# Layer 2 of a four-layer graph stack: the logit row and the transposed attention matrix go through DRAM and VectorE instead of TensorE

## The chip, the core and the metric

The kernel runs on one core of a Trainium2 chip, in float32. A core has five engines with a queue each, worked through strictly in order: TensorE (PE, matrix products; PEld is its weight load), VectorE (DVE), ScalarE (ACT), GpSimd (POOL) and SyncE (SP), which here does nothing but issue DMAs. The metric is the device time of one execution in microseconds (us); less is better.

## The reference, cut to what matters

`x` is 128 graphs ("batches") of 128 nodes by 512 features; `adj` is one 128 by 128 matrix for all. Each layer is `x = layernorm(x + layer(x))`:

```python
# layer 0: max over nodes of relu(A + C - A')           (adj as both weights)
# layer 1: 8-head attention masked by adj, projections Wq Wk Wv Wo
# layer 2: graph attention
h  = einsum('bnc,cf->bnf', x, W)
s1 = einsum('bnf,f->bn', h, a1);  s2 = einsum('bnf,f->bn', h, a2)
e  = leaky_relu(s1[:, :, None] + s2[:, None, :], 0.2) * mask      # mask is adj
att = softmax(e, axis=2)
out = elu(einsum('bij,bjf->bif', att, h) + beta * h)
# layer 3: norm_adj @ (x @ weight) + bias
```

In layer 2, `s1` is one number per row node and `s2` one number per column node. A column of 128 numbers lies across the 128 partitions of the on-chip memory, so `s2` has to be turned into a row that every partition holds. And the 128 by 128 matrix `att + beta * I` has to be transposed before TensorE can multiply by it. These two turnings are what the change is about.

## The kernel before, in words

The work on each batch is cut into named steps (a table `STEPS`, line 185). Each step has an engine, a cost that the author gave it, the steps that must precede it, and the buffers it takes. A planner in the kernel (`list_order`, line 74) walks through all steps of all 128 batches with these costs and writes down one order of work. On TensorE it takes the step that can start first, and among those the one of lowest `rank` (line 392): the batch number plus a lag given by stage (`LAG`, line 369), with a few exceptions (`LEAD`). The chip then follows this order, engine by engine; steps on different engines are tied by semaphores alone. So the order is fixed when the program is built, and each engine waits where its next instruction is not ready, however much else could be done.

Batches go in pairs (even and odd). The projections Q, K, V (layer 1), Y (layer 1's output), U (layer 2's weight) and Z (layer 3's weight) of a pair are computed with seven products in place of eight, steps `QP1` to `QP7` and so on, each about 0.9 us of TensorE; sums of blocks for them are formed by GpSimd (`US1` to `US4`), and results are evacuated from the accumulators by VectorE and ScalarE (`QU2`, `KU3`, `UC22`). The last six batches use the plain product (`YF0`, `YF1`, ...). `A` is layer 0's product, `SC` the attention scores and `O` the weighted values of layer 1, `GT` layer 2's product with the attention matrix, `NX` layer 3's with `norm_adj`. `MX1`/`MX2` write the normed batch to DRAM and read it back in another order of 32 by 32 blocks, which VectorE then transposes in place (`TX`); `MS1`/`MS2`/`TS` do the same with the attention weights of layer 1.

Layer 2 of a batch `b` runs in this order:

- `Y1`, `Q1`, `P1`, `AP1`: the layer norm behind layer 1 (VectorE, ScalarE, GpSimd, ScalarE).
- `L` (VectorE, line 1062): two dot products per node give the columns `s1` and `s2`.
- `E` (TensorE, line 1076): a transpose against the identity of `s2`, broadcast along the row, leaves the row of `s2` on all partitions, in an accumulator bank.
- `EZ` (ScalarE, line 1082): adds `s1`, twice: once into a buffer `z` in on-chip memory, once in place in the bank.
- `E1` (VectorE), `EE` (ScalarE), `E2` (VectorE): leaky relu, mask, maximum; exponential and its sum; division and `beta * I`.
- `BT` (TensorE, line 1115): transposes the matrix into a bank. `BE` (ScalarE, line 1120) copies it to a buffer `bT`.
- `GT` (TensorE, line 1125): eight matrix instructions; then `GE`, the sums, `UP1` to `UP7`, and the elu.

`E` and `BT` need a bank of the accumulator pool `ps` (five banks). The buffer counts are in `POOLS`: one `z`, two `bT`, two `e`, three pairs of `x2` (layer 1's result).

Of the kernel before, what the change touches and what calls it, by code (L numbers as in the profile page):

```python
# [8 lines left out]
F32 = mybir.dt.float32  # L9
AF = mybir.ActivationFunctionType  # L10
# [3 lines left out]
P = 128  # L14
S = 32
Q = P // S
# [55 lines left out]


def list_order(steps, rank, pools, n):
    todo = {(s, b) for s in steps for b in range(n) if steps[s].batches(b)}
    missing, users, ready = {}, {}, {}
# [12 lines left out]
    while todo:  # L89
        best = None  # L90
        for k in can:
            s = steps[k[0]]
            t = max(ready[k], free.get(s.engine, 0.0), free.get("port", 0.0) if s.port else 0.0)
            for i, (p, _) in enumerate(s.buffers(k[1])):
                n_taken = len(taken[p]) + (i and p == s.buffers(k[1])[i - 1][0])
                if n_taken >= pools[p]:
                    for r in taken[p][n_taken - pools[p]]:
                        t = max(t, ends.get(r, 1e9) + SIGNAL)
            if t >= 1e9:
                continue  # L100
            if s.engine != "PE":
                key = (t, ready[k] - s.soon - (s.rush if k[1] < 4 else 0.0), k, t)
            elif mode and s.mode:
                near = CLOSE + (CLOSE if s.mode == mode else 0.0)
                key = (max(t - AWAIT, free["PE"]), rank(*k) - near, k, t)
            else:
                key = (t, rank(*k), k, t)
            if best is None or key < best:
                best = key
# [63 lines left out]
def normed(b):  # L173
# [3 lines left out]
POOLS = {  # L177
    "ps": 5, "sc": 3, "x": 4, "xB": 2, "xT": 2,
    "qT": 2, "kT": 1, "v": 2, "s": 1,
    "sB": 2, "oT": 1, "x2": 3, "z": 1, "e": 2, "bT": 2, "gT": 1, "m": 1, "x3": 2,  # L180
    "nx": 1, "dx": 8, "dp": 2, "S": 2, "SX": 2, "u": 2, "uL": 1,
    "t0": 3, "t1": 3, "t2": 3, "t3": 3, "r": 3,
}
# [46 lines left out]
    "P1": Step("POOL", 0.58, "Q1", soon=20, batches=normed),  # L230
    "AP1": Step("ACT", 1.03, "P1", "P1*", soon=20),
    "L": Step("DVE", 1.45, "AP1", "LOG2a@", "LOG2b@", soon=20, port=True),
    "E": Step("PE", 0.12, "L", takes={"ps": ("E1",)}),
    "EZ": Step("ACT", 0.42, "E", takes={"z": ("E1",)}, soon=20),
    "E1": Step("DVE", 1.0, "EZ", takes={"e": ("BT",)}, soon=20),
    "EE": Step("ACT", 0.42, "E1", soon=20),
    "E2": Step("DVE", 0.57, "EE", soon=20, port=True),
    "BT": Step("PE", 0.12, "E2", takes={"ps": ("BE",), "bT": ("GT",)}),
    "BE": Step("ACT", 0.2, "BT", soon=20),
    "GT": Step("PE", 0.89, "BE", "GT-1", takes={"ps": ("GE",), "gT": ("U+",)}),  # L240
    "GE": Step("ACT", 0.5, "GT", soon=20),
    "UE": Step("ACT", 0.55, "U1", soon=20),
# [110 lines left out]
for n, need, weights, end, out in (  # L353
# [13 lines left out]


LAG = {
    "A": 0.692, "QP4": 9.305, "QP6": 13.674, "KP4": 14.013, "QP1": 14.257, "VP6": 14.264,  # L370
    "QP7": 14.272, "KP7": 14.275, "QP2": 14.757, "KP6": 14.810, "QP5": 16.139,
    "KP1": 16.167, "SC": 16.245, "QP3": 16.292, "KP5": 16.483, "KP2": 16.726, "KP3": 16.957,
    "VP1": 17.469, "VP7": 17.505, "VP2": 17.717, "VP4": 17.842, "VP3": 17.872,
    "VP5": 17.926, "YP4": 18.786, "YP5": 19.034, "O": 20.374, "YP3": 21.316, "YP1": 21.809,
    "YF1": 21.819, "YP2": 21.908, "YP6": 21.936, "YP7": 22.056, "E": 22.106, "UF1": 22.207,
    "YF0": 22.911, "BT": 23.043, "UP1": 23.223, "GT": 23.299, "UP4": 23.974, "UP5": 24.264,
    "UP3": 24.731, "UP2": 24.753, "UP6": 24.814, "UP7": 24.920, "UF0": 25.326,
    "ZP7": 25.453, "ZF0": 25.880, "NX": 25.925, "ZP4": 26.433, "ZP2": 26.459, "ZP6": 26.533,
    "ZP1": 27.158, "ZP3": 27.371, "ZP5": 27.563, "ZF1": 28.500,
}  # L380

LEAD = {
    "V55": -0.01, "NX59": 0.02, "GT60": -2.5, "V60": 0.06, "BT61": 0.07, "Z61": -1.43,
    "BT62": -0.59, "GT63": 1.52, "NX63": -0.85, "A4": 3.8, "O0": 1.06, "O1": -0.73, "GT2": 0.02,
    "V1": -0.26,
}


BOTH = range(128)


def rank(name, b):
    if name not in LAG:
        return -1.0
    stage = name[0] if name[1:2] in "PF" else name
    if name in ("SC", "O") and b in BOTH:
        b |= 1
    return b + LAG[name] - LEAD.get(f"{stage}{b // 2}", 0.0)


@with_exitstack
def kernel(
# [20 lines left out]
    nc = tc.nc  # L423
# [11 lines left out]
    dram = ctx.enter_context(  # L435
        tc.tile_pool(name="dram", bufs=2, space=bass.MemoryType.DRAM)
    )
# [4 lines left out]
    def mm_tile(name):  # L442
        return psum.tile([P, 512], F32, tag="ps", name=name, bufs=POOLS["ps"])

    def tr_tile(name):
        return mm_tile(name).rearrange("p (c f) -> p c f", c=C)

    def buf(tag, shape, b):
        return work.tile(shape, F32, tag=tag, name=f"{tag}_{b}", bufs=POOLS[tag])
# [73 lines left out]
    ident = const.tile([P, P], F32, tag="ident", name="ident")  # L523
# [103 lines left out]
    scores, probs, sums, dp, sT, v, oT = {}, {}, {}, {}, {}, {}, {}  # L627
    x2, s12, e, bT, gT, m, x3, nx = ({} for _ in range(8))
# [444 lines left out]
                accum_out=s12[b][:, i : i + 1],  # L1073
            )

    def E(b):

        ps = tr_tile(f"ps_e_{b}")
        nc.tensor.transpose(ps[:, 0, :], s12[b][:, 1:2].to_broadcast([P, P]), ident)
        e[b] = ps  # L1080

    def EZ(b):
        z = e[b][:, 0, :]
        s1 = s12.pop(b)[:, 0:1]
        z_sb = buf("z", [P, P], b)
        nc.scalar.activation(z_sb, z, AF.Identity, bias=s1)
        nc.scalar.activation(z, z, AF.Identity, bias=s1)
        e[b] = z, z_sb

    def E1(b):  # L1090
# [21 lines left out]
        )  # L1112
        e[b] = t

    def BT(b):
        ps = tr_tile(f"ps_bT_{b}")
        nc.tensor.transpose(ps[:, 0, :], e.pop(b), ident)
        bT[b] = ps

    def BE(b):  # L1120
        t = buf("bT", [P, P], b)
        nc.scalar.copy(t, bT[b][:, 0, :])
        bT[b] = t

    def GT(b):

# [84 lines left out]
    def OUT(b):  # L1211
# [3 lines left out]
    do |= {f.__name__: f for f in (  # L1215
        Q0, Q1, Q2, Q3,
        LD, ST0, A, R, P0, AP0, MX1, PX, PT, PTE, MX2, RL, C1, TX, SC, M0, M, SM1, EXP, SMR, SMN, MS1, MS2, TS, O, OE,
        Y1, P1, AP1, L, E, EZ, E1, EE, E2, BT, BE, GT, GE, U1, UE, U2, UP, U3, P2, AP2, NX, NE,
        C3, Z1, P3, AP3, OUT,
    )}  # L1220
    for name in FETCH:
# [55 lines left out]
```

## Time and profile before

| | |
|---|---|
| Time, median of 3 runs (lowest, highest) | 3055.86 us (3053.38, 3056.8) |
| Span of the profiled execution, first to last instruction | 3055.6 us |
| PE busy | 3021.9 us, 21062 instructions |
| DVE busy | 2350.8 us, 5379 instructions |
| ACT busy | 2215.0 us, 7240 instructions |
| POOL busy | 1624.7 us, 1907 instructions |
| Bytes moved by DMA, mean rate | 313.19 MB, 102 GB/s |
| Start of the score blocks of two successive pairs, late in the run | 2243.10 and 2289.79 us |

The profiled execution's span is 0.3 us below the median of the runs, so the sums can be made against either. Busy time is the time in which an engine has an instruction under way. Matrix instructions are pipelined: one that is "0.27 us" long from its first to its last moment can be followed by the next after 0.11 us. What a matrix instruction costs TensorE is therefore read from the distance between its start and the start of the next, not from its duration. In a timeline line, consecutive instructions of one kind are drawn together ("x8").

### The profile page before, as it was taken

How to read it: one execution, taken by the hardware profiler on the slowest of the kernel's cores; microseconds unless marked ns; L12 is line 12 of the kernel's file. 1: busy time of each engine (PE TensorE's matmuls, PEld its weight loads, DVE VectorE, ACT ScalarE, POOL GpSimd, SP SyncE). 2: the span in 40 equal slices, each digit the busy share in tenths (PEclk: the TensorE clock that was granted, in tenths of full speed). 3: DMA queues.
4: the chain of work that ended last, by engine and by line, in shares of the span. 5: the costliest groups of instructions: out<-in, count | busy, mean ns of one | idle time of the engine just before them, and what ended most of it. 6: DMA issues, size and time to landing. Idle time of an engine off the chain costs nothing.

```text
span 3055.6 us, 61911 instructions
## 1 busy us (share of the span) xinstructions
PE 3021.9 (99%) x21062; PEld 2706.8 (89%) x21062; DVE 2350.8 (77%) x5379; ACT 2215.0 (72%) x7240; POOL 1624.7 (53%) x1907
## 2 busy tenths in 40 slices
PE   7999999999999999999999999999999999999998
PEld 5888988988989989989889899898898898999987
DVE  6878777787787787877777877878778777777774
ACT  4677777777777776777777777777777777667675
POOL 4336555455455555554554655545545545556544
PEclk8999999999999999999999999999999999999999
DMA  7523333233233332332332323323323333223221
GB/s 198 179 87 124 89 107 111 85 116 104 84 118 98 97 114 88 111 108 83 118 102 91 117 88 107 111 87 115 104 84 118 98 97 109 86 77 97 70 84 38
DMA packets 235276, 313.19 MB, mean 102 GB/s; under 512 B 27729, under 2 KB 157649, under 8 KB 234961
## 3 DMA queue, kind: packets, MB, share of 16 engines
q1 hardware_dynamic: 233184, 308.19, 31.9%
q8 instruction: 167, 2.74, 0.4%
q10 hardware_dynamic: 1776, 1.05, 0.2%
q14 instruction: 149, 1.21, 0.1%
HBM read 174.92 MB, written 134.22 MB: 101 GB/s over the span
## 4 chain that ended last, share of the span: by engine, by line
PE 94%; DVE 3%; DMA 2%; ACT 1%; issue 0%; SPq 0%; POOL 0%; ACTq 0%; POOLq 0%; DVEq 0%
PE py_Q L737 6%; PE py_K L737 5%; PE py_U L737 5%; PE py_Y L737 5%; PE py_V L737 5%; PE py_Z L737 5%; PE ps_s L945 4%; PE pz_Q L737 4%; PE px_K L737 4%; PE pz_K L737 4%; PE ps_o L1024 4%; PE ps_nx L1181 4%; PE px_Q L737 4%; PE ps_gT L1130 4%; PE px_Z L737 4%; PE pz_V L737 4%
## 5 line engine op out<-in xcount | busy, mean ns | idle before, releaser
L1195 POOL TENSOR_TENSOR x<-x,b_bc 128x512 f32<-128x512 f32 x128 | 162.8, 1273 | 601.7 <-PE ps_nx L1181 601.6
L672 ACT ACTIVATE x<-x,off,rstd 128x512 f32<-128x512 f32 x512 | 416.8, 814 | 17.1
L981 ACT ACTIVATE s<-s,mx 128x128 f32<-128x128 f32 x1024 | 396.1, 390 | 36.7 <-DVE mx L975 36.6
L640 DVE BATCH_NORM_STATS2 st<-x 128x6 f32<-128x512 f32 x512 | 346.6, 677 | 13.9 <-POOL x L1162 7.7
L995 ACT ACTIVATE s<-s,sm 128x128 f32<-128x128 f32 x1024 | 313.3, 389 | 18.5 <-DVE sm L990 7.8
L667 POOL TENSOR_TENSOR rstd<-rstd,neg_half 128x2 f32<-128x2 f32 (+1 forms) x265 | 182.3, 688 | 149.9 <-ACT rstd L653 149.7
L1162 POOL TENSOR_TENSOR x<-x,x 128x512 f32<-128x512 f32 x128 | 163.2, 1275 | 142.4 <-DVE rs L1108 75.4
L716 POOL TENSOR_TENSOR SX_V<-xT 128x256 f32<-128x256 f32 x128 | 93.7, 732 | 272.2 <-PE py_Y L737 243.8
L1034 ACT COPY nx<-ps_nx 128x512 f32<-128x512 f32 x128 | 74.9, 585 | 215.9 <-PE ps_nx L1181 215.6
L1066 DVE SCALAR_TENSOR_TENSOR junk<-x,wa_bc 128x512 bf16<-128x512 f32 x256 | 207.1, 809 | 14.8 <-ACT x L672 4.0
L796 DVE TENSOR_TENSOR x<-py_U,u_U 128x256 f32<-128x256 f32 x183 | 77.6, 424 | 151.8 <-PE py_U L737 151.3
L981 ACT ACTIVATION_READ_ACCUMULATOR s<-s,mx 128x1 f32 x1024 | 193.5, 189 | 0.0
L959 DVE TENSOR_TENSOR s<-ps_s,mask 128x512 f32<-128x512 f32 x256 | 169.1, 682 | 9.3 <-DMA dp<-s 5.8
L896 POOL TENSOR_TENSOR x<-x,bo_bc 128x512 f32<-128x512 f32 x128 | 160.3, 1274 | 14.5 <-DVE bo_bc L593 8.1
L716 POOL TENSOR_TENSOR S_U<-gT 128x256 f32<-128x256 f32 x122 | 93.0, 762 | 128.8 <-ACT gT L1034 128.6
L1016 DVE STREAM_TRANSPOSE sB<-sB 128x1024 f32<-128x1024 f32 x128 | 157.9, 1234 | 0.8 <-DMA sB<-dp 0.8
L737 PEld LDWEIGHTS px_K<-xT,wk_sb 128*128 128x128 f32 x1024 | 133.8, 192 | 27.3 <-issue 23.6
L671 ACT ACTIVATE off<-off,rstd 128x1 f32<-128x1 f32 x512 | 145.6, 284 | 15.4 <-POOL rstd L667 15.2
L975 DVE TENSOR_REDUCE mx<-s 128x8 f32<-128x1024 f32 x128 | 153.5, 1199 | 0.3
L945 PE MATMUL ps_s<-kT,qT 64*128 64x128 f32 x2048 | 148.8, 285 | 0.0
L945 PEld LDWEIGHTS ps_s<-kT,qT 64*128 64x128 f32 x2048 | 124.3, 187 | 23.4 <-issue 23.1
L854 PE MATMUL ps_a<-x,adjT 128*128 128x512 f32 x256 | 134.4, 609 | 6.5 <-DMA x<-in_x 6.5
(190 smaller groups left out, 9151.1 us busy)
## 6 DMA issues: line engine op xcount, KB each, us to landing
dp<-s SPq DMA_DIRECT2D x128, 512.0 KB, 2.9
sB<-dp SPq DMA_DIRECT2D x512, 128.0 KB, 3.1
x<-in_x SPq DMA_DIRECT2D x128, 256.0 KB, 3.4
dx<-x SPq DMA_DIRECT2D x128, 256.0 KB, 4.4
x<-dx SPq DMA_DIRECT2D x64, 512.0 KB, 4.0
out_x<-x SPq DMA_DIRECT2D x128, 256.0 KB, 2.0
xB<-dx SPq DMA_DIRECT2D x496, 64.0 KB, 2.0
wo_sb<-in_L_gnn_Wo SPq DMA_DIRECT2D x5, 256.0 KB, 3.7
```

Of the source, the lines that this page charges most:

```text
L640: nc.vector.bn_stats(st, t)
L667: nc.gpsimd.tensor_tensor(r, r, neg_half.to_broadcast([P, r.shape[1]]), ALU.pow)
L672: nc.scalar.activation(dst, src, AF.Identity, bias=shift, scale=scale)
L716: nc.gpsimd.tensor_tensor(s[:, i], x, y, op)
L737: nc.tensor.matmul(to, lhsT=one, rhs=two, start=(new and k == 0), stop=(k == 1), skip_group_check=True,)
L945: nc.tensor.matmul(scores[b][par][:, c, :], lhsT=qT[b][rows, c, cols], rhs=kT[b][rows, c, cols], start=True, stop=True,)
L959: nc.vector.tensor_tensor(by_head(probs[b])[:, par * C : (par + 1) * C], scores[b][par].rearrange("p h (q s) -> p h q s", s=S), mask.rearr ...
L981: nc.scalar.activation(s[:, :, h], s[:, :, h], AF.Exp, bias=mx[:, h : h + 1], accum_out=sums[b][:, h : h + 1],)
L995: nc.scalar.activation(s[:, :, h], s[:, :, h], AF.Identity, scale=sm[:, h : h + 1])
L1066: nc.vector.scalar_tensor_tensor(junk, x2[b][:, b % 2], 1.0, wa_bc[i], op0=ALU.mult, op1=ALU.mult, accum_out=s12[b][:, i : i + 1],)
L1162: nc.gpsimd.tensor_tensor(t, t, x2.pop(b)[:, b % 2], ALU.add)
L1195: nc.gpsimd.tensor_tensor(t, t, b3_bc, ALU.add)
```

## The change

`E` and `BT` are taken out of TensorE.

- The row of `s2` now goes through DRAM: `ER1` writes the column to a DRAM tile of 128 numbers (one 4-byte element per partition), and `ER2` reads it back with every partition reading all 128 numbers, straight into `z`. Both are DMAs issued by SP. `EZ` still makes its two copies with `s1` added; it now reads `z` and takes its accumulator bank itself.
- The attention matrix goes through DRAM too: `BM1` writes it out (64 KB), `BM2` reads it back with four DMAs, each of which fills 32 partitions with 4 by 32 by 32 blocks in an order in which only the blocks themselves remain to be transposed (runs of 32 numbers, 128 bytes). `BE` is now VectorE's 32 by 32 transpose, in place, instead of ScalarE's copy out of a bank.
- The ranks are new: three tables by stage, for the first eight batches (`EARLY`), the last eight (`LATE`) and the rest (`LAG`), and no exceptions by pair. With them the order of nearly all steps changes.

```diff
-    "E": Step("PE", 0.12, "L", takes={"ps": ("E1",)}),
-    "EZ": Step("ACT", 0.42, "E", takes={"z": ("E1",)}, soon=20),
-    "E1": Step("DVE", 1.0, "EZ", takes={"e": ("BT",)}, soon=20),
+    "ER1": Step("SP", 0.4, "L", takes={"de": ("ER2",)}, dma=(1.6, 0.2)),
+    "ER2": Step("SP", 0.4, "ER1", takes={"z": ("E1",)}, dma=(1.6, 0.4)),
+    "EZ": Step("ACT", 0.72, "ER2", takes={"ps": ("E1",)}, soon=20),
+    "E1": Step("DVE", 1.0, "EZ", takes={"e": ("BM1",)}, soon=20),
...
-    "BT": Step("PE", 0.12, "E2", takes={"ps": ("BE",), "bT": ("GT",)}),
-    "BE": Step("ACT", 0.2, "BT", soon=20),
+    "BM1": Step("SP", 0.4, "E2", takes={"db": ("BM2",)}, dma=(1.6, 0.3)),
+    "BM2": Step("SP", 1.9, "BM1", takes={"bT": ("GT",)}, dma=(3.4, 1.0)),
+    "BE": Step("DVE", 0.24, "BM2", soon=20),
...
-    stage = name[0] if name[1:2] in "PF" else name
-    if name in ("SC", "O") and b in BOTH:
-        b |= 1
-    return b + LAG[name] - LEAD.get(f"{stage}{b // 2}", 0.0)
+    lag = (EARLY if b < 8 else LATE if b >= 120 else LAG)[name]
+    return (b | 1 if name in ("SC", "O") else b) + lag
...
-    def E(b):
-        ps = tr_tile(f"ps_e_{b}")
-        nc.tensor.transpose(ps[:, 0, :], s12[b][:, 1:2].to_broadcast([P, P]), ident)
-        e[b] = ps
+    def ER1(b):
+        e[b] = dram.tile([1, P], F32, tag="de", name=f"de_{b}", bufs=POOLS["de"])
+        nc.sync.dma_start(out=e[b].rearrange("o p -> p o"), in_=s12[b][:, 1:2])
+
+    def ER2(b):
+        row = buf("z", [P, P], b)
+        nc.sync.dma_start(out=row, in_=e[b].partition_broadcast(P))
+        e[b] = row
 
     def EZ(b):
-        z = e[b][:, 0, :]
-        s1 = s12.pop(b)[:, 0:1]
-        z_sb = buf("z", [P, P], b)
-        nc.scalar.activation(z_sb, z, AF.Identity, bias=s1)
-        nc.scalar.activation(z, z, AF.Identity, bias=s1)
+        z_sb, s1 = e[b], s12.pop(b)[:, 0:1]
+        z = tr_tile(f"ps_e_{b}")[:, 0, :]
+        nc.scalar.activation(z, z_sb, AF.Identity, bias=s1)
+        nc.scalar.activation(z_sb, z_sb, AF.Identity, bias=s1)
         e[b] = z, z_sb
...
-    def BT(b):
-        ps = tr_tile(f"ps_bT_{b}")
-        nc.tensor.transpose(ps[:, 0, :], e.pop(b), ident)
-        bT[b] = ps
+    def BM1(b):
+        bT[b] = dram.tile([P, P], F32, tag="db", name=f"db_{b}", bufs=POOLS["db"])
+        nc.sync.dma_start(out=bT[b], in_=e.pop(b))
+
+    def BM2(b):
+        t = buf("bT", [P, Q, S], b)
+        src = bT.pop(b)
+        for j in range(Q):
+            nc.sync.dma_start(
+                out=t[j * S : (j + 1) * S],
+                in_=src[:, j * S : (j + 1) * S].rearrange("(i s) f -> s i f", s=S),
+            )
+        bT[b] = t
 
     def BE(b):
-        t = buf("bT", [P, P], b)
-        nc.scalar.copy(t, bT[b][:, 0, :])
-        bT[b] = t
+        t = bT[b] = bT[b].rearrange("p q s -> p (q s)")
+        nc.vector.transpose(t, t)
```

The instruction order of the changed kernel, which is fixed when it is built, puts the new steps of an even batch (60 as the example) as follows. SP issues `ER1`, `ER2`, then `BM1` and `BM2` of batch 60, then `MS2` of batches 64 and 65. ScalarE has `EZ` of 60 behind the evacuations of `QP1` of pair 68. VectorE has `E1` of 60 just before the evacuation of `QP6` of pair 68, `E2` of 60 just behind the evacuation of `UP5` of pair 58, and `BE` of 60 behind the elu of 58. TensorE has `GT` of 60 behind the first two Z products of pair 56.

## The prediction

> **What bounds the kernel now.** I read the page's busy times first, then the chain that ended last.
>
> ```profile
> PE 3021.9 (99%) x21062; PEld 2706.8 (89%) x21062; DVE 2350.8 (77%) x5379; ACT 2215.0 (72%) x7240; POOL 1624.7 (53%) x1907
> ...
> PE 94%; DVE 3%; DMA 2%; ACT 1%; issue 0%; SPq 0%; POOL 0%; ACTq 0%; POOLq 0%; DVEq 0%
> ```
>
> TensorE is busy all the time and carries 94% of the chain. Busy alone could still hide waits shorter than an instruction, so I looked at the windows (columns: stretch, its length, busy time of PE, PEld, DVE, ACT, POOL, granted clock, DMA share, GB/s) and at all that TensorE waited for.
>
> ```profile
> 100.00:200.00 100.00, 98.50 (x723) 85.42 (x724) 79.51 (x184) 78.09 (x285) 35.10 (x46) 1.00 0.41 131
> 200.00:1500.00 1300.00, 1298.53 (x9146) 1168.37 (x9145) 1016.36 (x2335) 963.34 (x3146) 702.03 (x831) 1.00 0.32 102
> 1500.00:2900.00 1400.00, 1398.44 (x9853) 1263.17 (x9852) 1086.81 (x2481) 1027.71 (x3365) 771.77 (x902) 1.00 0.31 98
> ...
> PE pz_V L737 <- DVE v L796: 2.4, 4, 1.1
> ```
>
> From 200 to 2900 us TensorE idles 3 us in all (1.47 and 1.56), at full clock. The longest wait that repeats, for VectorE's evacuation of V, is 2.4 us over the whole run. So the time in this stretch is the sum of TensorE's issue slots, and what leaves TensorE leaves the time, unless a new wait takes its place. The slots are in the timeline of TensorE (start, length, instruction):
>
> ```profile
> 1540.68 1.03 PE L737 MATMUL pz_U<-w_sb,S_U 128*128 128x256 f32 x4
> 1541.54 0.27 PE L1117 MATMUL ps_bT<-ident,e 128*128 128x128 f32 x1
> 1541.65 0.27 PE L1079 MATMUL ps_e<-ident,s 128*128 128x128 f32 x1
> 1541.85 1.16 PE L945 MATMUL ps_s<-kT,qT 64*128 64x128 f32 x16
> 1542.95 1.97 PE L1024 MATMUL ps_o<-sB,v 128*64 128x128 f32 x32
> 1544.84 1.16 PE L945 MATMUL ps_s<-kT,qT 64*128 64x128 f32 x16
> 1545.93 1.13 PE L737 MATMUL px_Z<-w_sb,nx 128*128 128x256 f32 x4
> 1546.90 1.03 PE L737 MATMUL py_Z<-ZT,S_Z 128*128 128x256 f32 x4
> 1547.77 1.03 PE L737 MATMUL px_Z<-w_sb,nx 128*128 128x256 f32 x4
> ```
>
> Starts are what counts. `BT` holds TensorE from 1541.54 to 1541.65, 0.11 us. `E` is followed after 0.20 us, but the next one is a score block of another operand shape (64*128): 0.09 of it is the change of shape. The same shows at 1545.93, where the first Z product after the scores takes 0.97 us and the next 0.87. Ordinary seven-product steps take 0.87 us (128x256) or 0.89 us (128x128).
>
> **The change part by part.**
>
> 1. *Removed from TensorE:* 128 `E` and 128 `BT` at 0.11 us: 256 x 0.11 = 28.2 us. `BT` has no cover to lose, since TensorE hardly idles.
>
> 2. *Order on TensorE.* Going through both orders, TensorE changes operand shape (ordinary, scores, values) 269 times before and 288 times after. At 0.09 to 0.10 us each: 19 x 0.10 = +1.9 us.
>
> 3. *New latency up to E1.* In the new order `L` of an even batch stands on VectorE behind the evacuation of a `KP7`, and its `E1` just before that of the second `QP6` on. Between the ends of these TensorE steps lie five steps of Q and K at 0.89, five of U at 0.87 and one A at 0.86: 9.7 us. In it must fit: the evacuation 0.4, `L` 1.55 (2 x 0.69 + 2 x 0.08 and gaps), `ER1`, `ER2`, `EZ` 0.6 (0.37 and 0.34, overlapping), and some 0.5 for five hand-overs; 6.6 us remain for two small DMAs. No such DMA is in the steady part of this trace. The nearest rows are the loads at the very start: a column of 128 four-byte elements took 2.47 us (`b_sb`), 64 KB in 128 rows of 512 bytes 2.27 (`adj_sb`). The ends are 2.0 us each (the fastest 256 KB store) and 3.8 each (`bq_sb` with 512 four-byte elements and `bo_bc`, among the weights). I take 2.5 and 2.3, nearest in shape, sum 4.8: hidden with 1.8 us to spare. At the slow ends, 7.6, it would be 1.0 us late.
>
> 4. *New latency from E2 to GT.* This is the narrowest place. `E2` of an even batch stands behind the evacuation of `UP5`; from that step's end to `GT` TensorE has QP7, UP3, QP4, NX (3.5 us), two score and two value blocks (4.1, by the starts 1541.85 to 1545.93), two Z products (0.97 and 0.87): 9.5 us. The chain in it: evacuation 0.4, `E2` 0.5 (0.15 and 0.35), `BM1`, `BM2`, `BE`, hand-overs 0.6. For the DMAs:
>
> ```profile
> dp<-s SPq DMA_DIRECT2D x128, 512.0 KB, 2.9
> sB<-dp SPq DMA_DIRECT2D x512, 128.0 KB, 3.1
> ...
> dx<-x SPq DMA_DIRECT2D x128, 256.0 KB, 4.4
> ...
> out_x<-x SPq DMA_DIRECT2D x128, 256.0 KB, 2.0
> xB<-dx SPq DMA_DIRECT2D x496, 64.0 KB, 2.0
> ...
> 1518.28 3.75 SPq L884 DMA_DIRECT2D xB<-dx  x8
> ```
>
> The last column of the first lines is from issue to landing; `dx<-x` is slow because it is issued right behind the 512 KB of `x<-dx`. `BM1` is a quiet store like `out_x`: 2.0. `BM2` is the pattern of `xB` with a quarter of the bytes: the last of four is issued 3 x 0.47 = 1.4 us after the first (3.75 us for eight) and lands 2.0 later: 3.4. `BE` is an eighth of the 1.23 us that the 128x1024 transpose takes, 0.15, up to the 0.29 of any 128x128 VectorE pass; I take 0.2. Sum 0.4 + 0.5 + 2.0 + 3.4 + 0.2 + 0.6 = 7.1 us against 9.5: hidden with 2.4 to spare. At the slow ends (4.4, and 1.4 + 3.1) it is 10.6 and `GT` waits 1.1 us. I take the quiet values because on SP nothing large stands between the two output stores ahead of `ER1` and `BM2`. The odd batch's `GT` stands some 17 us of TensorE work further back, its `BM1` only behind the eight issues of `MS2`.
>
> 5. *Queues.* SP gets 7 more issues per batch on 12.5; at 0.47 us each 3.3 us on 5.9, of some 23.4 us that a batch takes. Behind `ER2` and `BM1`, which wait for landings, stand `MS2` of the layer-1 weights and `BM1` of the odd batch. `MS2` waits for `O` to free its buffer (1017.3 us of SP's waits are for that), and `O` is some 90 us of TensorE work behind its scores, so a microsecond there is covered. ScalarE loses `BE`, 128 x 0.257 = 33 us, and VectorE gains about 26 us on 2351; neither is the bound. DMA bytes grow by 25 MB on 313, its share from 0.32 to below 0.4.
>
> 6. *Fill and drain.* The first 13 TensorE steps are the same in both orders. The new row and matrix paths are longer by about 9 us in series (4.8 + 5.4 of DMA for two TensorE passes of 0.27 and `BE`'s 0.26). Where another batch's products fill in, that is free; at the drain it may not be. The old drain idles 1.2 us before the last product ends at 3048.4 and 7.2 after; the last batch's `GT` stands 21.8 us of TensorE work behind its Y product in the new order, against 19.6 us of rows in series (3.7 for the norm, 1.6 for `L`, 4.8 for the row, 2.5 for `EZ` to `E2`, 5.6 for matrix and `BE`, 1.4 for hand-overs): it just fits. I take 0, with -1.2 to +9 for the drain and -1.5 (the idle of 100 to 200 us) to +9 for the fill.
>
> Sum against the profiled execution: 3055.6 - 28.2 + 1.9 = 3029.3, so **3029 us**; the median of the runs is 0.3 us above that execution, which changes nothing.
>
> Two rules of the Trainium skill speak against this change. The page "VectorE: DVE Perf Modes", section "The three transpose paths", calls a plain DMA that transposes by strides 19 times slower than the crossbar's transposing DMA (put there at 1309 ns for 128 by 128) where the innermost destination stride is large; by it `BM2` would take an estimated 24.9 us, `GT` of every even batch would wait about 19 us, and the time would pass 4000 us. This trace's `xB` does such a block-wise read in 2.0 us, since whole runs and no single elements are moved, and the row decides. `ER1` does move single elements: the page "DMA: Bandwidth & Descriptors", section "Specifications", says that below 512 bytes the engine reads, modifies and writes; it gives no price, and no run here shows such a store.
>
> **The rivals.**
>
> *A: the matrix comes late (slower than before).* `GT` of the 61 even batches in pairs waits for `BE`, and TensorE with it. It begins when `BM1` and `BM2` together exceed 7.8 us and cancels the gain at 28.2 - 1.9 = 26.3 us, 0.43 us per pair, so at 8.2 us. At the slow rows (8.9) the wait is 1.1 x 61 = 67 us: 3096. For it speaks that `dx<-x` shows 4.4 us behind another transfer; against it the quiet SP order.
>
> *B: the row comes late.* `EZ` holds up ScalarE and `E1` VectorE, both with evacuations behind them. At 1.0 us late, QP7 needs the evacuation of QP6 some 1.8 us after that step, of which the evacuation itself takes 0.7: TensorE feels little, at most 0.2 x 61 = 12 us: 3041. At 5 us for `ER1` alone it would be a rival like A.
>
> *C: the new order is not as tight.* The pair distances of before are 46.69 us with exceptions that sum to some 5 us; these can go (3024), or as many more come, with the fill or the drain at its upper bound: 3029 + 5 + 9 = 3043.
>
> *D: it frees nothing, because TensorE waits elsewhere:* 3055. Against it the 3 us of idle in 2700.
>
> **How the numbers follow.** The forecast with its own spread (3022 to 3036) gets 0.66, C's upper part 0.10, B 0.09, A 0.12, D 0.03. The measurement tells 0.2%, 6 us, from no change. A ends slower except for its beginning (0.01 same, 0.01 faster); D is same; the rest is faster: 0.86, 0.04, 0.10. The range leaves A and D out and reaches to C's upper end and a little further, 3018 to 3046.
>
> **What would show it.** Right: pairs 46.3 us apart, no PE wait for `bT` and none for evacuations that grew, `BM1` near 2.0 and `BM2` at most 2.2 from issue to landing, PE busy 28 us less. Step 4 is wrong if PE waits for `bT` some 60 times; step 3 if ScalarE or VectorE wait for the `z` DMA; step 6 if the last 100 us show new idle time.

## The result and the profile after

The changed kernel takes 3519.41 us (median; 3515.15 to 3521.68) against 3056.33 us of the kernel before on the same chip: a ratio of 1.151, with a 95% interval from 1.150 to 1.153. The forecast was 3029 us, the range 3018 to 3046. The change loses 463 us where a gain of 27 was forecast.

The span of the profiled execution is 3513.4 us. Its page shows these busy times and, below them, the chain that ended last:

```profile
PE 3167.7 (90%) x20806; PEld 2808.8 (80%) x20806; DVE 2368.8 (67%) x5507; ACT 2181.7 (62%) x7112; POOL 1612.2 (46%) x1907
...
PE 66%; DMA 23%; DVE 7%; ACT 3%; issue 1%; SPq 0%; POOL 0%; ACTq 0%; POOLq 0%; DVEq 0%
```

TensorE has 256 instructions less, as it should, and yet is busy for 146 us more; it carries 66% of the chain instead of 94%, and DMA carries 23%. The chain by line names the DMAs: `de<-s` (`ER1`) 13.7% and `z<-de` (`ER2`) 8.5%. The waits of the changed kernel tell the same from the other end (engine, line and tile waited for; us in total, times, longest):

```profile
ACT ps_e L1106 <- DMA z<-de: 539.8, 124, 10.6
DVE ps_e L1113 <- ACT z L1107: 367.2, 75, 7.9
...
PE py_Q L755 <- DVE qT L807: 231.6, 53, 7.3
```

and its list of DMAs gives the size (KB each, median us from issue to landing):

```profile
z<-de SPq DMA_DIRECT2D x128, 64.0 KB, 3.7
db<-e SPq DMA_DIRECT2D x128, 64.0 KB, 2.5
bT<-db SPq DMA_DIRECT2D x512, 16.0 KB, 1.7
de<-s SPq DMA_DIRECT2D x128, 0.5 KB, 7.1
```

The smallest of these four, 512 bytes, takes the longest: 7.1 us at the median and 6.39 at the least. The load of 512 bytes at the start (`b_sb`) takes 2.4 us in the same list. One pair in the timeline shows how that reaches TensorE (start, length, instruction; the idle time before it and what ended it in brackets; SP, then ScalarE, VectorE and TensorE):

```profile
2004.63 1.87 SPq L1096 DMA_DIRECT2D de<-s  x2
2011.85 6.31 SPq L1100 DMA_DIRECT2D z<-de  x2
...
2016.68 0.37 ACT L1106 ACTIVATE ps_e<-z,s 128x128 f32<-128x128 f32 x1 [6.57 <-DMA z<-de]
...
2017.52 0.30 DVE L1113 SCALAR_TENSOR_TENSOR ps_e<-z,ps_e 128x128 f32<-128x128 f32 x1 [5.50 <-ACT z L1107]
...
2018.38 0.42 DVE L807 SCALAR_TENSOR_TENSOR qT<-py_Q,u_Q 128x256 f32<-128x256 f32 x1
...
2013.17 1.03 PE L755 MATMUL pz_U<-w_sb,S_U 128*128 128x256 f32 x4
2018.85 2.08 PE L755 MATMUL py_Q<-SX_V,QT 128*128 128x128 f32 x8 [4.65 <-DVE qT L807]
2020.72 1.92 PE L755 MATMUL pz_U<-w_sb,S_U 128*128 128x256 f32 x4
2022.42 1.91 PE L755 MATMUL py_Q<-xT,QT 128*128 128x128 f32 x8
```

`ER1` is issued at 2004.63, `ER2` can only follow at 2011.85, and the row is there at 2016.68. `EZ` waits for it on ScalarE and `E1` on VectorE, and behind `E1`, in VectorE's fixed order, stands the evacuation of a Q product (`qT`, 2018.38). Its bank is what TensorE needs next, so TensorE stands still for 4.65 us. And the wait is not all: the following products take 1.9 to 2.1 us instead of 1.05. The windows of the same stretch say why (us, busy time of PE, PEld, DVE, ACT and POOL, granted clock with 1.00 for full speed, DMA share, GB/s):

```profile
2005.00:2013.17 8.17, 8.17 (x54) 7.42 (x53) 4.25 (x12) 1.89 (x6) 0.00 (x0) 1.00 0.04 1
2013.17:2018.85 5.68, 1.03 (x7) 0.58 (x5) 1.27 (x5) 1.64 (x6) 0.00 (x0) 0.91 0.04 13
2018.85:2024.13 5.28, 5.28 (x20) 4.92 (x21) 2.32 (x8) 1.88 (x6) 0.00 (x0) 0.50 0.17 37
2024.13:2031.00 6.87, 6.87 (x80) 6.18 (x80) 4.78 (x7) 4.29 (x16) 4.58 (x5) 0.96 0.17 55
```

After the wait the granted clock is 0.50 for 5.3 us, which costs another 2.6. The 0.91 and 0.96 of the rows around it amount to 1.0 us at half clock before the wait ends and 0.5 behind, so the whole stretch of half clock is 6.8 us long; of the 68 such stretches in this trace 44 last 6.8 us and 22 last 3.4. That fits the Trainium skill, "TensorE: Matmul & The Clock Gate", section "Part 1: The HAM clock gate (the "warmup" mystery)", which has the clock halved after at least one idle window of about 3.4 us and restored after at least one busy window of the same length. Over the 53 waits for `qT` the mean is 4.4 us of waiting (231.6 by 53) and 4.6 us of half clock behind it, which costs 2.3: together 6.7. Successive pairs are 53.6 us apart at the median, 7.0 more than the 46.56 of the first experiment below, where neither occurs.

### The profile page after: what moved, and what is told of

It is laid out like the page before. It is cut to its first block, busy times and chain, and to the rows that moved or that the text cites. A ratio compares the mean times of both kernels' runs of the same rounds, so it can differ in the third digit from the quotient of the medians.

```text
span 3513.4 us, 63024 instructions
## 1 busy us (share of the span) xinstructions
PE 3167.7 (90%) x20806; PEld 2808.8 (80%) x20806; DVE 2368.8 (67%) x5507; ACT 2181.7 (62%) x7112; POOL 1612.2 (46%) x1907
## 3 DMA queue, kind: packets, MB, share of 16 engines
q10 hardware_dynamic: 1776, 1.05, 0.2%
## 4 chain that ended last, share of the span: by engine, by line
PE 66%; DMA 23%; DVE 7%; ACT 3%; issue 1%; SPq 0%; POOL 0%; ACTq 0%; POOLq 0%; DVEq 0%
DMA de<-s 14%; DMA z<-de 9%; PE py_Q L755 5%; PE py_V L755 5%; PE py_Y L755 4%; PE py_Z L755 4%; PE ps_s L963 4%; PE ps_gT L1159 3%; PE py_K L755 3%; PE ps_o L1042 3%; PE ps_nx L1210 3%; PE px_Z L755 3%; PE pz_V L755 3%; PE pz_Q L755 3%; PE px_Y L755 3%; PE pz_Z L755 3%
## 5 line engine op out<-in xcount | busy, mean ns | idle before, releaser
L1106 ACT ACTIVATE ps_e<-z,s 128x128 f32<-128x128 f32 x128 | 47.5, 371 | 539.8 <-DMA z<-de 539.8
L755 PE MATMUL py_Q<-SX_V,QT 128*128 128x128 f32 x1024 | 181.2, 334 | 197.2 <-DVE qT L807 197.2
L755 PEld LDWEIGHTS py_Q<-SX_V,QT 128*128 128x128 f32 x1024 | 165.2, 239 | 220.4 <-DVE qT L807 212.1
L1113 DVE SCALAR_TENSOR_TENSOR ps_e<-z,ps_e 128x128 f32<-128x128 f32 x128 | 37.4, 292 | 367.5 <-ACT z L1107 367.2
L1084 DVE SCALAR_TENSOR_TENSOR junk<-x,wa_bc 128x512 bf16<-128x512 f32 x256 | 185.0, 723 | 13.1 <-ACT x L690 2.2
L755 PE MATMUL pz_U<-w_sb,S_U 128*128 128x256 f32 x488 | 169.7, 484 | 10.7 <-DVE e L1115 6.5
L1159 PEld LDWEIGHTS ps_gT<-bT,x 128*128 128x128 f32 x1024 | 129.8, 192 | 26.3 <-issue 22.0
```

The source lines that it names most:

```text
L755: nc.tensor.matmul(to, lhsT=one, rhs=two, start=(new and k == 0), stop=(k == 1), skip_group_check=True,)
L1084: nc.vector.scalar_tensor_tensor(junk, x2[b][:, b % 2], 1.0, wa_bc[i], op0=ALU.mult, op1=ALU.mult, accum_out=s12[b][:, i : i + 1],)
L1159: nc.tensor.matmul(ps[:, c, :], lhsT=x2[b][:, b % 2, c * P : (c + 1) * P], rhs=t, start=True, stop=True,)
```

## The experiments

All kernels keep the changed kernel's order of steps, but for the one step that run 5 moves, so that they differ only in what is named. The short diffs, cut to what matters, are against the changed kernel.

**1. The row with a quick store.** The second dot product of `L` is put into the first column of a 128x32 tile, VectorE's 32x32 block transpose (0.21 us) lays it into four rows, and `ER1` stores four runs of 128 bytes. Same bytes, same place in DRAM.

```diff
-                accum_out=s12[b][:, i : i + 1],
+                accum_out=s12[b][:, :1] if i == 0 else cols[b % 4][:, :1],
             )
+        t = e[b] = cols[b % 4]
+        nc.vector.transpose(t, t)
...
-        nc.sync.dma_start(out=e[b].rearrange("o p -> p o"), in_=s12[b][:, 1:2])
+        nc.sync.dma_start(out=e[b].rearrange("o (i s) -> (o i) s", s=S), in_=t[0:P:S, :])
```

> The changed kernel in its own order of steps, with one store replaced: L puts its second dot product into the first column of a 128x32 tile, VectorE turns that tile's 32x32 blocks in place, and ER1 then stores four runs of 128 bytes instead of 128 single numbers. Same result. Theory S (the 4-byte stores of the column to DRAM are what came late: 7.1 us instead of the 2.5 I took): de<-s lands in about 2 us, z<-de in about 2.8, sum 4.8 inside the 6.6 us of room; the pairs return to 46.3 us, the time to about 3030 (3020 to 3045). Theory T (any way of the row through DRAM is too late, since two landings stand in series and z<-de alone took 3.7): the store gains 5 us, ScalarE still waits for z one or two us per pair, 3100 to 3300. Theory O (the new order is too tight, or the matrix is late): nothing much changes, 3450 or more.

Measured: 3044.65 us (3043.77 to 3046.49), ratio 0.9963 (0.9949 to 0.9977), span 3042.8. From `ER1`'s issue to `ER2`'s are now 2.1 us (7.2 in the changed kernel); the odd batch's `ER1` stands between the two, so the store takes 2.1 at most. The trace of this run has no landing times for these transfers. Its timeline of SP and its page:

```profile
2031.69 2.04 SPq L1102 DMA_DIRECT2D de<-col  x2
2033.82 5.56 SPq L1106 DMA_DIRECT2D z<-de  x2
```

```profile
PE 3004.8 (99%) x20806; PEld 2684.0 (88%) x20806; DVE 2381.6 (78%) x5639; ACT 2173.0 (71%) x7112; POOL 1613.0 (53%) x1907
```

With this one store replaced all of the loss is gone: TensorE's busy time falls from 3167.7 to 3004.8 us and its idle time (span less busy) from 345.7 to 38.0. So of the 470.6 us between the two spans, 308 were waiting and 163 were slower instructions. Half clock accounts for most of the 163: by the clock records TensorE was busy for 309 us at half clock in the changed kernel, which costs 154, and for 10 us in this run. Everything else of the change, the matrix by DRAM, the new ranks and the queues, is in this kernel too.

It is not yet 3029. Pairs are 46.56 us apart, not 46.25. The missing 0.31 shows in the timeline at `GT` of an even batch (SP, then VectorE, GpSimd and TensorE):

```profile
2041.95 0.32 SPq L1143 DMA_DIRECT2D db<-e  x1
2043.53 1.74 SPq L1150 DMA_DIRECT2D bT<-db  x4
...
2041.58 0.35 DVE L1136 SCALAR_TENSOR_TENSOR e<-e,rs,beta_id 128x128 f32<-128x128 f32 x1
...
2048.93 1.39 DVE L1136 SCALAR_TENSOR_TENSOR e<-e,rs,beta_id 128x128 f32<-128x128 f32 x1
2050.24 0.30 DVE L1158 STREAM_TRANSPOSE bT<-bT 128x128 f32<-128x128 f32 x1
...
2048.90 1.27 POOL L1197 TENSOR_TENSOR x<-x,x 128x512 f32<-128x512 f32 x1 [0.81 <-DVE rs L1134]
...
2049.53 1.03 PE L758 MATMUL py_Z<-ZT,S_Z 128*128 128x256 f32 x4
2050.64 1.13 PE L1165 MATMUL ps_gT<-bT,x 128*128 128x128 f32 x8
```

`GT` starts 1.11 us after the Z product whose slot is 0.87: 0.24 late, and its own slot is 0.07 long. It waits for `BE` (`bT`, 2050.24 to 2050.54). The DMAs are not to blame: the last quarter was issued before 2045.3, and a quarter takes 1.7 us to land in the changed kernel. `BE` stands on VectorE behind `E2` of the *odd* batch, and that one takes 1.39 us where `E2` of the even batch takes 0.35; GpSimd's addition of 1.27 us runs at the same time.

**2. The matrix by DRAM alone.** The row is turned by TensorE again, directly ahead of `EZ`.

```diff
     def ER1(b):
...
+        pass
...
     def ER2(b):
...
+        pass
...
     def EZ(b):
...
+        ps = tr_tile(f"ps_e_{b}")
+        nc.tensor.transpose(ps[:, 0, :], s12[b][:, 1:2].to_broadcast([P, P]), ident)
+        e[b] = ps
```

> The changed kernel in its own order, with the row turned on TensorE again: E stands directly ahead of EZ, ER1 and ER2 do nothing; the matrix still goes through DRAM. Theories S and T: 128 slots of 0.11 us come back, 3029 + 14 = 3043, and up to 15 more since EZ now waits a few tenths for the transpose and its bank (3040 to 3060). Theory O: TensorE still waits for the matrix or for evacuations, 3300 or more.

Measured: 3058.95 us (3057.73 to 3060.12), ratio 1.0008 (0.9999 to 1.0017), pairs 46.78 us apart. The distances add up: 46.25, two `E` of 0.11 each, and the same 0.31 at `GT`. The row's transposes are worth 0.22 of a pair, and with the store repaired the row path costs TensorE nothing in the middle of the run.

**3 and 4. What in the store is slow?** Run 3 lets each partition store 16 numbers (64 bytes) instead of one; run 4 one number of 4 bytes as before, but with 64 bytes from one to the next in DRAM, in a fixed tile of 128x16.

```diff
-        nc.sync.dma_start(out=e[b].rearrange("o p -> p o"), in_=s12[b][:, 1:2])
+        e[b] = dram.tile([P, 16], F32, tag="de", name=f"de_{b}", bufs=POOLS["de"])   # run 3
+        nc.sync.dma_start(out=e[b], in_=s12[b])                                      # run 3
...
+        e[b] = de[b % 4]                                                             # run 4
+        nc.sync.dma_start(out=e[b][:, 0:1], in_=s12[b][:, 1:2])                      # run 4
```

> The changed kernel, with ER1 storing 16 numbers (64 bytes) per partition instead of one, and ER2 reading the first 128 numbers of that tile: the row then holds other numbers than s2, so this kernel leaves the right row out and only its times count. If the price is that of the store's size (a store smaller than some unit of the memory is dear, theory S1): de<-s falls to 2 to 3 us and the time to 3030 to 3060. If it is the price of 128 separate descriptors (S2): de<-s stays near 7 us and the time near 3510.

> The changed kernel, with ER1 storing one 4-byte number per partition, but 64 bytes apart in DRAM (into a tile zeroed once at the start), and ER2 reading the first 128 numbers of the tile: again not the right row, only the times count. If what is slow is that 16 neighbouring 4-byte stores fall into the same 64 bytes and wait for each other (S3): de<-s falls to 2 to 3 us and the time to 3030 to 3060. If a 4-byte store to DRAM is slow by itself (S1): about 7 us and 3510.

Measured, one execution each: 3041.57 us with the 64-byte stores, 3042.25 with the spaced numbers, pairs 46.56 in both. The list of DMAs of run 4:

```profile
z<-de SPq DMA_DIRECT2D x128, 64.0 KB, 2.9
...
de<-s SPq DMA_DIRECT2D x128, 0.5 KB, 1.4
```

The same 128 elements of 4 bytes land in 1.4 us instead of 7.1 when they are not neighbours in DRAM. Neither the number of elements nor their size is slow; where they are written decides. And `z<-de` is 2.9 instead of 3.7 by itself: in the changed kernel the even batch's read (4.6 at the median, the odd one's 2.8) is issued while the odd batch's store is still under way; here the two are 3.0 and 2.8.

**5. `BE` earlier on VectorE.** Run 1 with `BE` of the even batch moved in the order from behind `E2` of the odd batch to just ahead of it.

```diff
-        for _, name, b in list_order(STEPS, rank, POOLS, B):
+        order = [(name, b) for _, name, b in list_order(STEPS, rank, POOLS, B)]
+        for b in range(0, B, 2):
+            be, e2 = order.index(("BE", b)), order.index(("E2", b + 1))
+            if 0 < be - e2 < 12:
+                order.insert(e2, order.pop(be))
+        for name, b in order:
             do[name](b)
```

> As e1 (four runs of 128 bytes instead of 128 single numbers), and in the order of steps BE of the even batch moved ahead of E2 of the odd batch, wherever it stood close behind it. In e1 each pair still takes 46.56 us where 46.25 were expected: GT of the even batch waits 0.24 + 0.07 us, because BE stands on VectorE behind the odd batch's division, which takes 1.39 us beside GpSimd's 1.27 us addition instead of 0.35. Theory P (that neighbour is the whole remainder): 0.31 x 45 pairs = 14 us less than e1, 3031 (3027 to 3035), pairs 46.25. Theory Q (the matrix's DMAs are late, or the order is short of room elsewhere): 3040 or more, pairs 46.5.

Measured: 3030.57 us (3029.46 to 3032.13), ratio 0.9915 (0.9902 to 0.9929), pairs 46.25 us apart. Page and timeline of this kernel:

```profile
PE 2994.3 (99%) x20806; PEld 2687.2 (89%) x20806; DVE 2370.4 (78%) x5639; ACT 2174.5 (72%) x7112; POOL 1614.9 (53%) x1907
```

```profile
2036.79 0.30 DVE L1158 STREAM_TRANSPOSE bT<-bT 128x128 f32<-128x128 f32 x1
...
2037.18 1.20 DVE L1136 SCALAR_TENSOR_TENSOR e<-e,rs,beta_id 128x128 f32<-128x128 f32 x1
...
2037.59 1.03 PE L758 MATMUL py_Z<-ZT,S_Z 128*128 128x256 f32 x4
2038.45 1.05 PE L1165 MATMUL ps_gT<-bT,x 128*128 128x128 f32 x8
```

`BE` now ends 1.4 us before `GT`, and `GT` follows the Z product after 0.86 us. TensorE is busy 2994.3 us, 27.6 less than before the change. This kernel, the change with a quick store and one VectorE step moved, is quicker than the kernel before and than run 1.

**6 and 11. The new order with both turnings on TensorE.** Run 6 puts `BT` and ScalarE's copy at the place of `BE`, run 11 `BT` at that of `BM1` and the copy at that of `BM2`. `E` stands directly ahead of `EZ` in both. The diff is run 11's.

```diff
     def BM1(b):
-        bT[b] = dram.tile([P, P], F32, tag="db", name=f"db_{b}", bufs=POOLS["db"])
-        nc.sync.dma_start(out=bT[b], in_=e.pop(b))
+        ps = tr_tile(f"ps_bT_{b}")
+        nc.tensor.transpose(ps[:, 0, :], e.pop(b), ident)
+        bT[b] = ps
...
     def BM2(b):
-        for j in range(Q):
-            nc.sync.dma_start(
...
+        t = buf("bT", [P, P], b)
+        nc.scalar.copy(t, bT[b][:, 0, :])
```

> The changed kernel's order of steps with both turnings on TensorE again: E directly ahead of EZ, BT directly ahead of ScalarE's copy at BE's place, no DMA of row or matrix. It tells what the new order is worth by itself. If order and ranks are neutral (my steps 2 and 6): 3055.6 + 1.9 and a few us for the two transposes' banks, 3055 to 3068. If the new order is worth more than the removed transposes: below 3050. If it is a loss: above 3075.

> The changed kernel's order of work with both turnings on TensorE again, now with the kernel before's distances: the logits' transpose directly ahead of EZ, the matrix's transpose at BM1's place just behind E2, ScalarE's copy at BM2's place. Theory that the order itself is neutral: 3050 to 3068 us, the kernel before's 3056 with the 0.31 us for each pair that the run with the matrix alone kept, and pairs of 46.7 to 46.9 us. Theory that the new ranks are what costs: over 3090 us with pairs over 47.3, as in the run before with both on TensorE (3143.6, 48.24).

Run 6 took 3143.6 us (3142.47 to 3144.14; ratio 1.0283, 1.0269 to 1.0297), pairs 48.24. TensorE waits there for the copy:

```profile
PE ps_gT L1153 <- ACT bT L1146: 54.3, 59, 1.5
```

`BT`, the copy and `GT` stand one behind the other at that place, so this run tests that placement and not the order by itself. Run 11 took 3091.89 us (3091.26 to 3092.49; ratio 1.0116, 1.0099 to 1.0133), pairs 47.28. The waits for `bT` are gone; another has come, here in the waits of run 11 and in its timeline (ScalarE, TensorE):

```profile
PE py_V L755 <- ACT gT L1052: 16.6, 51, 0.3
```

```profile
2034.84 0.58 ACT L1052 COPY gT<-ps_gT 128x512 f32<-128x512 f32 x1
...
2033.11 1.05 PE L1154 MATMUL ps_gT<-bT,x 128*128 128x128 f32 x8
2034.00 0.27 PE L1138 MATMUL ps_bT<-ident,e 128*128 128x128 f32 x1
2034.11 1.03 PE L755 MATMUL px_V<-wv_sb,xT 128*128 128x256 f32 x4
2035.47 1.13 PE L755 MATMUL py_V<-VT,SX_V 128*128 128x256 f32 x4 [0.33 <-ACT gT L1052]
```

A V product is 0.49 late and 0.10 longer: 46.25 + 4 x 0.11 + 0.59 = 47.28. It does not read `gT`; what it can wait for is the bank that the copy gives back. In run 5, without `BT`, ScalarE's copy of `gT` starts as long after `GT`'s start (2038.45 and 2040.18, here 2033.11 and 2034.84: 1.73 us) and the V product follows without a gap, so the bank that `BT` takes in between is the likely cause; no run shows that by itself. So with both turnings on TensorE the new order is not neutral; the time lies just past the bound of the theory that it costs (3090 us), the pairs just short of its 47.3, both far below run 6. It costs 35 us, by a wait that the change itself does not have.

**7 to 10. How far apart must the numbers be?** As run 4, with 16, 32, 4 and 8 bytes from one number to the next (tiles of 4, 8, 1 and 2 columns). Run 9, at 4 bytes, is the changed kernel's store again, but into a fixed 128x1 tile and without the rearranged view.

```diff
+    de = [dram.tile([P, 4], F32, tag=f"de{i}", name=f"de{i}", bufs=1) for i in range(4)]
...
-        nc.sync.dma_start(out=e[b].rearrange("o p -> p o"), in_=s12[b][:, 1:2])
+        e[b] = de[b % 4]
+        nc.sync.dma_start(out=e[b][:, 0:1], in_=s12[b][:, 1:2])
```

> As e4 (one 4-byte number per partition, row not the right one, only times count), with 16 bytes between the numbers in DRAM instead of 64: four numbers share 64 bytes. If the stores wait for each other in steps of the shared 64 bytes: de<-s between 1.4 (pitch 64) and 7.1 us (pitch 4), about 2.5, and the time still near 3042. If only the 512 bytes of the whole column matter: 1.4 us as at pitch 64.

> As e7 with 32 bytes between the numbers, two in each 64 bytes. In steps of the shared 64 bytes: about 1.8 us; if the unit is 32 bytes: 1.4 us as at pitch 64. The time near 3042.

> Row as in the changed kernel, 128 numbers of 4 bytes at neighbouring addresses of DRAM, but into one of four fixed 128x1 tiles that are set to zero at the start, with no rearranged view of a 1x128 tile; the same 512 bytes, and the row is the right one. Theory pitch (the neighbouring addresses are slow, whoever writes them): the store lands after 7 us as in the changed kernel, the time is 3500 to 3530 us. Theory form (the slow thing is the rearranged destination or the fresh tile): the store lands after 1.4 us as at 16, 32 and 64 bytes, the time is 3038 to 3050 us.

> The same with the numbers 8 bytes apart in a tile of 128x2; the row read back is then not the logit row, so the output is not the reference's. Theory pitch with a step between neighbours and others: 1.4 us and 3038 to 3050 us. Theory pitch that grows with the numbers in one stretch of DRAM: between 1.4 and 7.1 us, so at 3.5 to 4 us a time of 3040 to 3250. Theory form: 1.4 us.

Measured, one execution each:

| bytes from number to number | `ER1` to landing, median | pairs, median | time |
|---|---|---|---|
| 4 (the changed kernel) | 7.1 us | 53.6 us | 3519.41 us |
| 4 (run 9) | 7.9 us | 54.55 us | 3608.0 us |
| 8 (run 10) | 3.1 us | 46.57 us | 3084.89 us |
| 16 (run 7) | 1.4 us | 46.57 us | 3048.38 us |
| 32 (run 8) | 1.4 us | 46.57 us | 3038.59 us |
| 64 (run 4) | 1.4 us | 46.56 us | 3042.25 us |

The lists of DMAs of run 9 and run 10:

```profile
de<-s SPq DMA_DIRECT2D x128, 0.5 KB, 7.9
```

```profile
de<-s SPq DMA_DIRECT2D x128, 0.5 KB, 3.1
```

Run 9 settles pitch against form: the store is slow without the rearranged view too. Its time is past what was expected, with a store that is 0.8 us slower still; why it is, stays open. My guess for run 7, a price set by how many numbers share 64 bytes, with 2.5 us at 16, was wrong: for this store nothing is left of it at 16 bytes. Between 16 and 4 bytes each halving of the distance more than doubles the time. The four stores that set the tiles to zero at the start, one after the other among the loads, go the same way: 11.1 us with 4 bytes to a partition, side by side (run 9), 5.8 with 8, 4.0 with 16, 2.0 with 32 and with 64. So 16 bytes were enough for one store in a quiet stretch, and not there.

Run 10 also shows where the schedule stands: 3.1 us for `ER1` and 3.2 for `ER2` are 6.3, within the forecast's 6.6 us of room, and pairs in the middle of the run are hardly held up (47.35 at the most). What run 10 loses against run 4 lies at the two ends: 20 us up to the scores of the ninth pair (386.7 against 366.4) and 20 after those of the 52nd (691.9 to the end against 671.6). TensorE idles more in both stretches (37.8 us against 21.3, and 25.0 against 11.4), for evacuations and for the first loads; which step sets that off is not shown.

## Why the prediction was wrong

**Step 3, the size of `ER1`, is the term that failed.** It was put at 2.5 us, with ends of 2.0 and 3.8; it measured 7.1. `ER2` was put at 2.3, and the even one measured 4.6. Against 6.6 us of room they are 11.7 together, 5.1 us late, where TensorE's wait in the pair shown is 4.65. With the numbers spaced (run 4) the two take 1.4 and 2.9, 4.3 against the 4.8 of the forecast. So the path of the wait and the room were read rightly, and the price of this store was not. The rows that I bounded it by were *loads* of small elements (`b_sb`, `bq_sb`), and quiet *stores* of whole rows. No row of the trace had 4-byte stores, let alone neighbouring ones. The loads touch the small elements in the other direction, so 3.8 was no upper end for this store, and the text had said that no run showed such a store. Nor was 3.8 the slow end of the loads. The same list of the kernel before has a second load of the same shape and size, and a third (`bv_sb`, 5.1):

```profile
bq_sb<-in_L_gnn_bq ACTq DMA_DIRECT2D x1, 2.0 KB, 3.8
bk_sb<-in_L_gnn_bk ACTq DMA_DIRECT2D x1, 2.0 KB, 5.2
```

With 5.2 for `ER1` the prediction's own condition for a rival like A ("At 5 us for `ER1` alone") was met by a row on hand. The working had the row late from 6.6 us on, and the chance of 0.09 for it rested on 3.8 as the upper end.

The Trainium skill's "DMA: Bandwidth & Descriptors", section "Specifications", with its reading, modifying and writing below 512 bytes, pointed at the right instruction. The section says this of a transfer's rate and gives no time to land. Size below 512 bytes is not by itself what the runs show to be slow: stores of 128 bytes (run 1), 64 bytes (run 3) and single 4-byte numbers 16 bytes apart (run 7) all land in time. What is slow is neighbours. Whether 4-byte stores that share a piece of DRAM wait for one another's modification there is a possible reading of 1.4, 3.1 and 7.1 us; no run looks into that.

**Rival B was the right mechanism with the wrong price.** It named `EZ` and `E1` with the evacuations behind them, and that "at 5 us for `ER1` alone it would be a rival like A". It was priced at 1.0 us late, where an evacuation's slack covers nearly all (3041). At 5.1 late the slack is gone, and each such wait brings 3.4 or 6.8 us of half clock with it. That second loss, most of 163 of 471 us, was in no case of the forecast: a wait was taken to cost its own length.

**Step 1 holds.** The 28.2 us of transposes are real: the pair distances of runs 1, 2 and 5 (46.56, 46.78 and 46.25) are sums of 46.25, 0.11 for each transpose kept and 0.31 for one wait, and 46.69 before is 46.25 and four times 0.11. With both sources of waiting gone (run 5) the time is 3030.57 against the forecast of 3029.

**Step 2** (1.9 us of shape changes) is not tested by itself; the traces have the 269 and 288 changes that it counted. Run 5's TensorE is busy 27.6 us less than before; the two steps together forecast 26.3.

**Step 4 was right on the DMAs and wrong on its end.** In the changed kernel `BM1` of an even batch takes 1.5 us at the median (forecast 2.0; the odd one's 2.9 makes the 2.5 of the list), a quarter of `BM2` 1.7 (2.0), so rival A never came by its DMAs: at 1.7 us the data of run 1 lie there more than 3 us before `BE`. But the chain left out what stands ahead of `BE` on VectorE, the odd batch's `E2`, and took every `E2` for 0.35. Beside GpSimd's addition that of the odd batch is 1.39, and `BE` is 0.30, not 0.2. That was to be seen in the kernel before, where the same operation has this row (ns, least, median and longest):

```profile
L1110 DVE SCALAR_TENSOR_TENSOR e<-e,rs,beta_id x128: 350/353/1398, 148.0 to 3010.5; 128x128 f32<-128x128 f32 x128
```

It costs 0.31 us per pair, 14 us from run 1 to run 5 (3044.65 to 3030.57, on two chips where the kernel before takes 3056.45 and 3056.89). So with a store at its forecast price the change would have taken 3042 to 3045 us (runs 1, 3 and 4): inside the range, but only by the width that was left for rival C. The wait is the one of rival A (`GT` for `BE`), its cause is one that no rival named; a hit would have been luck.

**Step 5** holds: `ER2` waits on SP for 461 us in all in the changed kernel, and past the first two loads of `x` (6.4 us of waits, 6.5 before) no wait of TensorE is for the tiles of `MS2` or the loads behind it. **Step 6** holds within its bounds as far as two marks tell: in run 5 the first scores start at 58.6 us (59.8 before), and from the last pair's scores to the end are 124.5 us (128.6 before).

**Rival C** has a grain of truth: the new order is tight for the change but leaves the old turnings no place (runs 6 and 11).

## What to carry to other kernels

A bound from the nearest row holds only if the row goes in the same direction: here the store of small elements was not priced by a load of them, and the slowest like row was passed over. Where the trace has no such row, the range must reach to the point where the schedule breaks. Here a column transposed in on-chip memory first (at most 2.1 us), or numbers 16 bytes apart in DRAM (1.4), replaced a store of 7.1 us. And a stall of TensorE of over 4 us is to be priced at its length and half the stretch of half clock behind it; before trusting a step's place, look at what stands directly ahead of it on its engine, at its longest duration and not its median.

## What the runs showed of the hardware that was not expected

- 128 stores of 4 bytes, one from each partition, land in 1.4 us (medians) when they are 16, 32 or 64 bytes apart in DRAM, in 3.1 us at 8 bytes and in 7.1 to 7.9 us when they are neighbours. The same 512 bytes as four runs of 128 bytes cost no more than the spaced ones in the schedule (pairs 46.56 us apart in both).
- A read of 512 bytes by all 128 partitions takes 2.8 us, and 4.6 when it is issued while another batch's neighbouring store is under way.
- One VectorE operation of two tensors and a scalar column (`E2`, 128x128) takes 0.35 us, and mostly 1.2 to 1.4 us while GpSimd adds. In the kernel before all 61 of the 128 that take over 0.7 us overlap an addition of 128x256 or 128x512 for at least 0.65 us; of the other 67 one overlaps for more than 0.1 us (0.45).
- After a wait of 4.65 us TensorE ran at a granted clock of 0.50 for 5.3 us. In the changed kernel each of its 65 waits of 3.6 us or more (from 40 us on) has half clock at its end or just behind it; the 59 waits of at most 1.5 us in run 6 have none.
